# The skip term D x of a state-space layer: from products with diagonal matrices on TensorE to a copy on ScalarE and a product and a sum on GpSimd

## The chip, the cores and the metric

The kernel runs on one core of one Trainium2 chip. The metric is the device time of one execution in microseconds (us), the median of three runs. A profile of one further execution is at hand. Its engines are called PE (TensorE's matrix products; PEld is its loading of the stationary operand), DVE (VectorE), ACT (ScalarE), POOL (GpSimd) and SP (SyncE, which here only issues DMAs).

## What is computed

Two transformer-like layers over x of shape 4 x 512 x 512, all in float32. Each half layer is x = x + f(g), where g is a gate computed by scans over time (a bidirectional WKV recurrence) and f is in turn a state-space layer (Mamba2), a mixture of 8 experts, attention, and a feed-forward layer. The change lies in the state-space layer, whose core is this (b rows, l tokens, 16 heads of 64 channels, 1024 inner channels, 128 states):

```python
x = xBC[..., :D_INNER].reshape(b, l, NHEADS, HEADDIM)
xdt = xc * dtc[..., None]
Y_diag = jnp.einsum('bcgls,bgHcls,bcsgHp->bclgHp', CB, Lmat, xdt)
states = jnp.einsum('bcsgn,bgHcs,bcsgHp->bcgHpn', Bc, decay_states, xdt)
Y_off = jnp.einsum('bclgn,bcgHpn,bgHcl->bclgHp', Cc, prev, jnp.exp(dA_cs))
y = (Y_diag + Y_off).reshape(b, l, NHEADS, HEADDIM) + x * D_skip[None, None, :, None]
y = y.reshape(b, l, D_INNER)
y = y * jax.nn.silu(z)
```

and then a norm over the 1024 channels and a projection back to 512. The skip term is `x * D_skip`: each head's channels times one number of that head.

## The kernel before

**Stages.** The kernel first makes the gates of the first row. Then comes the state-space stage, which ends in the profile at about 720 us and overlaps the experts from about 660 us; then the experts, attention, and the feed-forward layer. During the state-space stage a generator (`make_gates`, stepped by `pump`) interleaves the gate work of seven further gates: scans on VectorE (L259, L265), products on VectorE (L254 to L331), exponentials and scalings on ScalarE. The gates are due one by one, where `have(...)` stands, the last two tiles before the end of the stage.

**Tiles, halves and groups.** The stage loops over 4 rows of the batch (`b`) and, in each, over 4 tiles of 128 tokens (`t`). Within a tile the 1024 channels are worked in two halves (`hh`) of 512, which are 8 heads. One tile's half is called a group here; there are 32. For each group the code calls

- `decays(u, hh)`: ScalarE makes the decay matrix `lm` of 8 heads (eight Relu at L1162, one Exp), VectorE multiplies it by `cb` (L1168), TensorE turns the convolved channels `xc`, which lie channel by token, into token by channel (`pxt`, four transposes, L1173), VectorE reads `pxt` twice for `xdt` and `xde` (L1177, L1181). Last, TensorE opens the sum `pyd` with four products of `xc` by `skip` (L1186); `skip` holds 8 diagonal 128 x 128 matrices with D on the diagonal, which GpSimd builds once at the start (L957).
- `outputs(u, hh)`: `pyo`, the product with the state (L1200), VectorE's scaling of it into `y` (L1201), eight products that end the sum `pyd` (L1203), VectorE's sum `y + pyd` (L1213), GpSimd's product by the gate `zs` (L1214). In a row's first tile there is no state, and one product on VectorE of `pyd` by `zs` (L1211) takes the place of these. Then the state is updated: `pst` (L1217), GpSimd's `st*ex` (L1222), VectorE's sum (L1223).
- `squares`, `norm`, `turn`, `project`, `scale`, `add_x`: the norm and the projection, one tile later, as `old`. `norm` is a chain of small GpSimd operations (L1232 to L1248) with one on VectorE (L1242).

**Order.** The code of one tile is written in the order `decays(u, 1)`, `outputs(u, 0)`, the norm of the tile before, `start_tile` and `start_scores` of the next, `decays(next, 0)`, `outputs(u, 1)`. The framework turns this text ahead of time into a fixed order for each engine, taking what stands earlier in the text first; `after(...)` holds some calls behind the last instruction of an engine. On the chip each engine then works through its own queue.

**Buffers.** Tiles with one tag share a ring of `bufs` buffers, and the next taker waits for the last reader of the oldest one. PSUM has three rings: `mm` (4 banks), `tp` (2 banks: transposes, `pxt` among them, and small products) and `acc` (2 banks: `pyd`, and the experts' `po`). In SBUF the rings of `xdt` and `xde` have 2 buffers, `y` has 3.

**Constants.** `cols` holds vectors as columns (one number per partition), `rows` holds vectors that are broadcast to all partitions; `heads(row, hh)` stretches 8 numbers, one per head, over 8 x 64 channels. Each of the two is loaded by one DMA on SP.

Of the kernel before, what the change touches and what calls it, by code (L numbers as in the profile page):

```python
# [10 lines left out]
F32 = mybir.dt.float32  # L11
# [3 lines left out]
ALU = mybir.AluOpType  # L15
# [3 lines left out]
P = 128  # L19
# [5 lines left out]
DI, DS, NH, HD, KC = 1024, 128, 16, 64, 4  # L25
CONV = DI + 2 * DS
NCV = CONV // P
NDI = DI // P
DPROJ = 2 * DI + 2 * DS + NH

E, I = 8, 512
# [27 lines left out]
    ("conv_w", NCV * KC),  # L59
    ("conv_b", NCV),  # L60
    ("norm_w", NDI),
    ("D_skip", NDI),
    ("gate_s", NFF),
    ("up_s", NFF),
    ("down_s", NC),
# [5 lines left out]
    _n += _w  # L71
NCOLS = _n

_ROWS = [("dt_bias", NH), ("A_log", NH), ("gate_b", E)]
_ROW = {}
_n = 0
for _name, _w in _ROWS:
# [6 lines left out]
def block_kernel(ctx: ExitStack, tc: tile.TileContext, a: dict, out: bass.AP):  # L84
    nc = tc.nc
# [51 lines left out]
    rt = ctx.enter_context(tc.tile_pool(name="moe_r", bufs=1))  # L137
# [11 lines left out]
    def ps_acc(name):  # L149
        return ps.tile([P, 512], F32, tag="acc", name=name, bufs=2)  # L150
# [7 lines left out]
    def col(name, i=0, n=1):  # L158
        lo = _COL[name][0] + i
        return cols[:, lo : lo + n]  # L160
# [5 lines left out]
    ident = const.tile([P, P], F32, name="ident")  # L166
# [307 lines left out]
    e_nq = count("e_nq", [[NQ, E]])  # L474
    v_id = count("v_id", [[1, 1]], 1)

    v_lo = rt.tile([P, 1], F32, name="v_lo")
    v_e = rt.tile([P, 1], F32, name="v_e")
    jk = rt.tile([P, E], F32, name="jk")
    nc.vector.tensor_tensor(jk, sel, e_nq, ALU.mult)  # L480
    nc.vector.tensor_reduce(v_e, jk, AX.X, ALU.add)
# [415 lines left out]
    with ExitStack() as ph:  # L897
# [3 lines left out]
        wz = ph.enter_context(tc.tile_pool(name="ssm_wz", bufs=1, reuse_waits="tile"))  # L901
        hp = ph.enter_context(tc.tile_pool(name="ssm_h", bufs=1, reuse_waits="tile"))
        sm = ph.enter_context(tc.tile_pool(name="ssm", bufs=1, reuse_waits="tile"))
# [48 lines left out]
        wzt = wz.tile([P, NC, DI], F32, name="wzt")  # L952
        wot = wz.tile([P, NDI, C], F32, name="wot")

        skip = wz.tile([P, NDI, P], F32, name="skip")
        for j in range(NDI):
            nc.gpsimd.tensor_scalar(skip[:, j, :], ident, col("D_skip", j), None, ALU.mult)  # L957
        for k in range(NC):
            nc.sync.dma_start(out=wxb[:, k, :], in_=a["in_projT"][k * P : (k + 1) * P, DI:])
        for k in range(NC):  # L960
# [170 lines left out]
        def start_scores(u):  # L1131
            w, t = u.w, u.t
            pp = ps_tp("pp")

            nc.tensor.matmul(pp[:, P : 2 * P], lhsT=w.Bc[:, u.tok], rhs=w.Cc[:, u.tok], start=True, stop=True)
            nc.tensor.transpose(pp[:, 2 * P : 3 * P], w.Bc[:, u.tok], ident)
            u.cb = sm.tile([P, P], F32, tag="cb", name="cb")
            nc.vector.tensor_tensor(u.cb, pp[:, P : 2 * P], tri_le, ALU.mult)
            u.bt = sm.tile([P, P], F32, tag="bt", name="bt", bufs=2)
            nc.scalar.copy(u.bt, pp[:, 2 * P : 3 * P])  # L1140
            u.ex, u.dte = w.ex[:, :, t, :], w.dte[:, t, :]
            u.ss = sm.tile([P, 2], F32, tag="ss", name="ss", bufs=2)
            u.xdt, u.xde, u.lm, u.pyd, u.y = [], [], [], [], []

        def load_sums(w, t, hh):

# [7 lines left out]
        def decays(u, hh):  # L1154

            w, t = u.w, u.t
            lm = w.lm.pop((t, hh))
            u.lm.append(lm)

            for i in range(8):  # L1160
                h = t * NH + hh * 8 + i
                nc.scalar.activation(  # L1162
                    lm[:, i, :], lm[:, i, :], AF.Relu, bias=w.cs[:, h : h + 1], scale=-1.0
                )
            lmf = lm.rearrange("p h l -> p (h l)")
            act(lmf, lmf, AF.Exp, scale=-1.0)
            for q in (slice(0, 4), slice(4, 8)):
                nc.vector.tensor_tensor(  # L1168
                    lm[:, q, :], lm[:, q, :], u.cb.unsqueeze(1).to_broadcast([P, 4, P]), ALU.mult
                )  # L1170
            pxt = ps_tp("pxt")
            for j in range(4):
                nc.tensor.transpose(  # L1173
                    pxt[:, j * P : (j + 1) * P], w.xc[hh * 4 + j][:, u.tok], ident
                )
            xdt = sm.tile([P, 512], F32, tag="xdt", name="xdt", bufs=2)
            nc.vector.tensor_tensor(split(xdt), split(pxt), heads(w.dt[:, t, :], hh), ALU.mult)  # L1177
            u.xdt.append(xdt)
            if not u.last:
                xde = sm.tile([P, 512], F32, tag="xde", name="xde", bufs=2)  # L1180
                nc.vector.tensor_tensor(split(xde), split(pxt), heads(u.dte, hh), ALU.mult)  # L1181
                u.xde.append(xde)

            pyd = ps_acc("pyd")
            for j in range(4):
                nc.tensor.matmul(  # L1186
                    pyd[:, j * P : (j + 1) * P], lhsT=w.xc[hh * 4 + j][:, u.tok],
                    rhs=skip[:, hh * 4 + j, :], start=(j == 0), stop=False,
                )
            u.pyd.append(pyd)  # L1190

        def outputs(u, hh):

            w, pyd = u.w, u.pyd[hh]
            ch = slice(hh * 512, (hh + 1) * 512)
            y = sm.tile([P, 512], F32, tag="y", name="y", bufs=3)
            u.y.append(y)
            if not u.first:
                pyo = ps_mm("pyo")
                nc.tensor.matmul(pyo, lhsT=w.Cc[:, u.tok], rhs=w.state[:, ch], start=True, stop=True)  # L1200
                nc.vector.tensor_tensor(split(y), split(pyo), heads(u.ex[:, 0, :], hh), ALU.mult)  # L1201
            for hd in range(8):
                nc.tensor.matmul(  # L1203
                    pyd[:, hd * HD : (hd + 1) * HD],
                    lhsT=u.lm[hh][:, hd, :],
                    rhs=u.xdt[hh][:, hd * HD : (hd + 1) * HD],
                    start=False,
                    stop=(hd == 7),
                )
            if u.first:  # L1210
                nc.vector.tensor_tensor(y, pyd, u.zs[hh], ALU.mult)  # L1211
            else:
                nc.vector.tensor_tensor(y, y, pyd, ALU.add)  # L1213
                nc.gpsimd.tensor_tensor(y, y, u.zs[hh], ALU.mult)  # L1214
            if not u.last:
                pst = ps_mm("pst")
                nc.tensor.matmul(pst, lhsT=u.bt, rhs=u.xde[hh], start=True, stop=True)  # L1217
                st = w.state[:, ch]
                if u.first:
                    nc.scalar.copy(st, pst)  # L1220
                else:
                    nc.gpsimd.tensor_tensor(split(st), split(st), heads(u.ex[:, 2, :], hh), ALU.mult)  # L1222
                    nc.vector.tensor_tensor(st, st, pst, ALU.add)  # L1223
# [75 lines left out]
        w = start_row(0)  # L1299
# [23 lines left out]
        u = start_tile(w, 0)  # L1323
# [6 lines left out]
        for b in range(B):  # L1330
# [6 lines left out]
            for t in range(NT):  # L1337
# [97 lines left out]
                old, u = u, nxt  # L1435
# [433 lines left out]
def _lay_out(n):  # L1869


    def chunks(v):

        return np.asarray(v).reshape(-1, P).T

    t = lambda v: np.ascontiguousarray(np.swapaxes(np.asarray(v), -1, -2))
    wkv = ("L0_cond", "L0_cond2", "L1_cond", "L1_cond2")
    w1, b1 = np.asarray(n["L0_ffn_w1"]), np.asarray(n["L0_ffn_b1"])
    cols = {
        "wkv_w": np.concatenate([chunks(n[f"{c}_w"]) for c in wkv], 1),  # L1880
        "wkv_u": np.concatenate([chunks(n[f"{c}_u"]) for c in wkv], 1),
        "condT": np.asarray(n["cond_512"]).T,
        "conv_w": np.asarray(n["L0_attn_conv_w"]).reshape(NCV, P, KC).transpose(1, 0, 2).reshape(P, -1),
        "conv_b": chunks(n["L0_attn_conv_b"]),
        "norm_w": chunks(n["L0_attn_norm_w"]),
        "D_skip": chunks(np.repeat(np.asarray(n["L0_attn_D_skip"]), HD)),
        "gate_s": chunks(n["L1_ffn_gate_s"]),
        "up_s": chunks(n["L1_ffn_up_s"]),
        "down_s": chunks(n["L1_ffn_down_s"]),
    }  # L1890
    rows = {
        "dt_bias": n["L0_attn_dt_bias"],
        "A_log": n["L0_attn_A_log"],
        "gate_b": n["L0_ffn_gate_b"],
    }
    by_part = lambda v: v.reshape(E, -1, P, v.shape[-1]).swapaxes(1, 2)
    w1x = np.stack([by_part(t(w1[:, i::2, :])) for i in range(2)], 2)
    got = {
        "cols": np.concatenate([cols[k] for k, _ in _COLS], 1),
        "rows": np.concatenate([np.asarray(rows[k]) for k, _ in _ROWS]),  # L1900
        "xT": np.asarray(n["x"]).transpose(2, 0, 1),
        "fT": np.asarray(n["fside_BxSxS_0"]).transpose(2, 0, 1),
        "in_projT": t(n["L0_attn_in_proj_w"]),
        "out_projT": t(n["L0_attn_out_proj_w"]),
        "gate_wT": t(n["L0_ffn_gate_w"]),
        "w1x": w1x.reshape(E, P, -1),
        "w2x": by_part(t(n["L0_ffn_w2"])).reshape(E, P, -1),
        "b1x": np.concatenate([b1[:, 0::2], b1[:, 1::2]], 1),
        "b2x": n["L0_ffn_b2"],
        "w_q": n["L1_attn_w_q"],  # L1910
        "w_kv": n["L1_attn_w_kv"],
        "w_dense": n["L1_attn_w_dense"],
        "gateT": t(n["L1_ffn_gate_w"]),
        "upT": t(n["L1_ffn_up_w"]),
        "downT": t(n["L1_ffn_down_w"]),
    }
    return {k: np.ascontiguousarray(v) for k, v in got.items()}
# [18 lines left out]
```

## Time and profile before

| | |
|---|---|
| median of three runs | 2333.18 us (2331.7 to 2336.78) |
| the profiled execution's own time | 2336.05 us |
| its span in the profile | 2334.3 us |
| granted TensorE clock, mean | 0.981 |
| the skip products at L1186 | from 101.4 to 652.9 us |

In the profile a float32 product of two 128 x 128 operands shows as two records, so the four skip products of a group are eight. The end of a TensorE record is modelled and lies after the start of the next; what a product costs TensorE is therefore read from start to start. Rows of busy time by stretch give: start and end, length, then for PE, PEld, DVE, ACT and POOL the busy us and the number of instructions, then the granted TensorE clock, the DMA engines' busy share and GB/s. Rows on waits give who waited, for whom, the total in us, how often, and the longest. Rows on one tile or line give the least, median and greatest duration in ns, and when the first and last one started.

### The profile page before, as it was taken

How to read it: one execution, taken by the hardware profiler on the slowest of the kernel's cores; microseconds unless marked ns; L12 is line 12 of the kernel's file. 1: busy time of each engine (PE TensorE's matmuls, PEld its weight loads, DVE VectorE, ACT ScalarE, POOL GpSimd, SP SyncE). 2: the span in 40 equal slices, each digit the busy share in tenths (PEclk: the TensorE clock that was granted, in tenths of full speed). 3: DMA queues.
4: the chain of work that ended last, by engine and by line, in shares of the span. 5: the costliest groups of instructions: out<-in, count | busy, mean ns of one | idle time of the engine just before them, and what ended most of it. 6: DMA issues, size and time to landing. Idle time of an engine off the chain costs nothing.

```text
span 2334.3 us, 24564 instructions
## 1 busy us (share of the span) xinstructions
PE 2201.7 (94%) x8148; PEld 1283.5 (55%) x8148; DVE 1463.2 (63%) x2846; ACT 1037.2 (44%) x2095; POOL 283.8 (12%) x306
## 2 busy tenths in 40 slices
PE   2879999999999899999899999999999999999999
PEld 1545565565655444444455555555555555558887
DVE  8698989999634566665466656555555544457332
ACT  4475675766712333242345544443444333343222
POOL 4023242332221111112100000000000000000000
PEclk9888999999999999999999999999999999999999
DMA  7442341622424368977622111011100000041100
GB/s 264 163 135 68 104 159 55 207 92 73 171 78 180 131 224 317 355 255 255 233 68 81 46 37 50 28 32 45 50 28 14 10 28 1 1 167 37 37 19 19
DMA packets 87653, 251.76 MB, mean 108 GB/s; under 512 B 9632, under 2 KB 18208, under 8 KB 78112
## 3 DMA queue, kind: packets, MB, share of 16 engines
q1 hardware_dynamic: 78656, 224.43, 28.2%
q0 software_dynamic: 6560, 21.50, 2.7%
q10 hardware_dynamic: 2304, 4.20, 0.5%
q8 instruction: 67, 1.10, 0.2%
q14 instruction: 66, 0.54, 0.1%
HBM read 285.09 MB, written 55.18 MB: 146 GB/s over the span
## 4 chain that ended last, share of the span: by engine, by line
PE 43%; DVE 4%; ACT 3%; issue 0%; DMA 0%; ACTq 0%
PE pd L1670 9%; PE pq L1606 7%; PE pctx L1655 6%; PE psc L1623 4%; PE pv L1592 2%; PE pk L1584 2%; PE ptp L1646 2%; PE pfo L1766 2%; PE pfo L1765 2%; PE pfg L1765 2%; PE pfg L1766 2%; PE pfu L1766 2%; PE pfu L1765 2%; DVE nmax L1628 1%; DVE num L259 1%; ACT pr L128 1%
## 5 line engine op out<-in xcount | busy, mean ns | idle before, releaser
L1606 PE MATMUL pq<-h,wq 128*128 128x512 f32 x512 | 245.5, 593 | 0.0
L1670 PE MATMUL pd<-cx,wd 128*128 128x512 f32 x512 | 223.0, 593 | 0.0
L1626 DVE TENSOR_TENSOR psc<-psc,mask 128x128 f32<-128x128 f32 x256 | 72.2, 287 | 191.7 <-PE psc L1623 191.3
L1048 PE MATMUL pc<-h,wxb 128*128 128x512 f32 x320 | 149.4, 623 | 43.6 <-DVE h L1307 38.7
L128 ACT ACTIVATE pr<-psc,nmax 128x128 f32<-128x128 f32 (+3 forms) x256 | 135.2, 529 | 104.0 <-DVE nmax L1628 103.0
L1678 DVE TENSOR_TENSOR xr<-xr,pd 128x512 f32<-128x512 f32 x64 | 44.0, 687 | 193.8 <-PE pd L1670 193.8
L1655 PE MATMUL pctx<-pT,v 128*128 128x512 f32 (+3 forms) x512 | 154.8, 446 | 8.4 <-ACT pT L1649 7.3
L1670 PEld LDWEIGHTS pd<-cx,wd 128*128 128x128 f32 x512 | 96.4, 191 | 115.1 <-issue 111.3
L1623 PE MATMUL psc<-kT,qT 128*128 128x128 f32 (+3 forms) x512 | 150.9, 435 | 3.2 <-ACT pr L128 2.4
L1655 PEld LDWEIGHTS pctx<-pT,v 128*128 128x128 f32 x512 | 94.4, 192 | 98.8 <-issue 38.4
L811 PE MATMUL pg<-w,hT 128*128 128x512 f32 x296 | 136.6, 603 | 6.8 <-ACT hT L784 6.8
L1614 ACT ACTIVATE qT<-pq 128x512 f32<-128x512 f32 x64 | 38.2, 598 | 233.6 <-PE pq L1606 233.6
L844 PE MATMUL po<-w,yT 128*128 128x512 f32 x296 | 135.8, 600 | 6.2 <-ACT yT L837 6.2
L822 PE MATMUL pn<-w,hT 128*128 128x512 f32 x296 | 133.4, 593 | 0.3 <-DMA w<-in_w1x 0.3
L1048 PEld LDWEIGHTS pc<-h,wxb 128*128 128x128 f32 x320 | 62.2, 199 | 116.2 <-issue 74.4
L1628 DVE TENSOR_REDUCE nmax<-psc 128x1 f32<-128x128 f32 (+3 forms) x256 | 123.4, 484 | 3.0
L1646 PEld LDWEIGHTS ptp<-ident,pr 128*128 128x128 f32 x640 | 77.7, 142 | 85.0 <-issue 41.6
L1606 PEld LDWEIGHTS pq<-h,wq 128*128 128x128 f32 x512 | 86.2, 191 | 53.6 <-issue 52.6
L1267 PE MATMUL po<-wot,yT 128*128 128x512 f32 x256 | 115.0, 603 | 0.0
L1119 PE MATMUL pz<-wzt,h 128*128 128x512 f32 x256 | 114.6, 596 | 0.3 <-ACT st L1220 0.3
L1623 PEld LDWEIGHTS psc<-kT,qT 128*128 128x128 f32 x512 | 86.2, 190 | 51.1 <-issue 25.8
L1646 PE MATMUL ptp<-ident,pr 128*128 128x128 f32 x640 | 96.1, 276 | 7.5 <-DVE pT L1649 4.0
(340 smaller groups left out, 4303.6 us busy)
## 6 DMA issues: line engine op xcount, KB each, us to landing
w<-in_w1x SPq DMA_DIRECT2D x76, 1024.0 KB
w<-in_w2x SPq DMA_DIRECT2D x38, 1024.0 KB
wb<-in_b1x SPq DMA_DIRECT2D x38, 512.0 KB
lm<-cs SPq DMA_DIRECT2D x32, 512.0 KB
kt<-in_fT SPq DMA_DIRECT2D x62, 256.0 KB
ek<-ek SPq DMA_DIRECT2D x62, 256.0 KB
ekv<-ekv SPq DMA_DIRECT2D x62, 256.0 KB
g<-num SPq DMA_DIRECT2D x30, 512.0 KB
```

Source lines behind the costliest of these rows:

```text
L128: nc.scalar.activation(*args, **kw)
L811: nc.tensor.matmul(pg, lhsT=hT[:, k, :], rhs=self.w1[s][0][:, k, :], start=(k == 0), stop=(k == NC - 1))
L844: nc.tensor.matmul(po, lhsT=yT[:, j, :], rhs=self.w2[s][:, j, :], start=(j == 0), stop=(j == NI - 1))
L1048: nc.tensor.matmul(pc, lhsT=wxb[:, k, m * P : (m + 1) * P], rhs=h[:, k, :], start=(k == 0), stop=(k == NC - 1),)
L1606: nc.tensor.matmul(pq, lhsT=u.wq[:, k, i * KVC : (i + 1) * KVC], rhs=u.h[:, k, :], start=(k == 0), stop=(k == NC - 1),)
L1623: nc.tensor.matmul(psc[:, :n], lhsT=qT[:, qi * P : n], rhs=u.kT[:, :n], start=True, stop=True)
L1628: nc.vector.tensor_reduce(nmax, psc[:, :n], AX.X, ALU.max, negate=True)
L1646: nc.tensor.transpose(ptp[:, kj * P : (kj + 1) * P], pr[:, kj * P : (kj + 1) * P], ident)
L1655: nc.tensor.matmul(pctx[:, kj * P :], lhsT=u.v[:, kj, :], rhs=pT[:, kj, kj * P :], start=(kj == 0), stop=(kj == NT - 1),)
L1670: nc.tensor.matmul(po, lhsT=u.wd[:, i, m * P : (m + 1) * P], rhs=u.ctxT[i], start=(i == 0), stop=(i == HPG - 1),)
L1765: nc.tensor.matmul(out_, lhsT=w, rhs=xs[0], start=first_, stop=False)
L1766: nc.tensor.matmul(out_, lhsT=w, rhs=xs[1], start=False, stop=last_)
```

## The change

The diagonal matrices go, and with them the four products of each group. Instead, in `decays`, ScalarE copies `pxt` from PSUM to a new SBUF tile `xs` (a ring of 2 buffers), and GpSimd multiplies it in place by D, broadcast over each head's channels. In `outputs`, GpSimd adds `xs` to `y` after VectorE's sum; in a row's first tile VectorE adds `xs` to `pyd`, where it multiplied `pyd` by `zs`. The product by `zs` is GpSimd's in every tile. `pyd` is taken from its ring in `outputs`, not in `decays`. D moves from `cols` (8 columns, repeated per channel) to `rows` (16 numbers, one per head). In SBUF, `skip` took 4 KB of a partition, and the two buffers of `xs` take 4 KB. `v_lo` and `v_e` of the routing become the two columns of one tile.

```diff
--- before.py
+++ after.py
@@ -59,7 +59,6 @@
     ("conv_w", NCV * KC),
     ("conv_b", NCV),
     ("norm_w", NDI),
-    ("D_skip", NDI),
     ("gate_s", NFF),
     ("up_s", NFF),
     ("down_s", NC),
@@ -71,7 +70,7 @@
     _n += _w
 NCOLS = _n
 
-_ROWS = [("dt_bias", NH), ("A_log", NH), ("gate_b", E)]
+_ROWS = [("dt_bias", NH), ("A_log", NH), ("D_skip", NH), ("gate_b", E)]
 _ROW = {}
 _n = 0
 for _name, _w in _ROWS:
@@ -474,8 +473,8 @@
     e_nq = count("e_nq", [[NQ, E]])
     v_id = count("v_id", [[1, 1]], 1)
 
-    v_lo = rt.tile([P, 1], F32, name="v_lo")
-    v_e = rt.tile([P, 1], F32, name="v_e")
+    v_both = rt.tile([P, 2], F32, name="v_both")
+    v_lo, v_e = v_both[:, 0:1], v_both[:, 1:2]
     jk = rt.tile([P, E], F32, name="jk")
     nc.vector.tensor_tensor(jk, sel, e_nq, ALU.mult)
     nc.vector.tensor_reduce(v_e, jk, AX.X, ALU.add)
@@ -952,9 +951,6 @@
         wzt = wz.tile([P, NC, DI], F32, name="wzt")
         wot = wz.tile([P, NDI, C], F32, name="wot")
 
-        skip = wz.tile([P, NDI, P], F32, name="skip")
-        for j in range(NDI):
-            nc.gpsimd.tensor_scalar(skip[:, j, :], ident, col("D_skip", j), None, ALU.mult)
         for k in range(NC):
             nc.sync.dma_start(out=wxb[:, k, :], in_=a["in_projT"][k * P : (k + 1) * P, DI:])
         for k in range(NC):
@@ -1140,7 +1136,7 @@
             nc.scalar.copy(u.bt, pp[:, 2 * P : 3 * P])
             u.ex, u.dte = w.ex[:, :, t, :], w.dte[:, t, :]
             u.ss = sm.tile([P, 2], F32, tag="ss", name="ss", bufs=2)
-            u.xdt, u.xde, u.lm, u.pyd, u.y = [], [], [], [], []
+            u.xdt, u.xde, u.lm, u.xs, u.y = [], [], [], [], []
 
         def load_sums(w, t, hh):
 
@@ -1180,18 +1176,14 @@
                 xde = sm.tile([P, 512], F32, tag="xde", name="xde", bufs=2)
                 nc.vector.tensor_tensor(split(xde), split(pxt), heads(u.dte, hh), ALU.mult)
                 u.xde.append(xde)
-
-            pyd = ps_acc("pyd")
-            for j in range(4):
-                nc.tensor.matmul(
-                    pyd[:, j * P : (j + 1) * P], lhsT=w.xc[hh * 4 + j][:, u.tok],
-                    rhs=skip[:, hh * 4 + j, :], start=(j == 0), stop=False,
-                )
-            u.pyd.append(pyd)
+            xs = sm.tile([P, 512], F32, tag="xs", name="xs", bufs=2)
+            nc.scalar.copy(xs, pxt)
+            nc.gpsimd.tensor_tensor(split(xs), split(xs), heads(row("D_skip"), hh), ALU.mult)
+            u.xs.append(xs)
 
         def outputs(u, hh):
 
-            w, pyd = u.w, u.pyd[hh]
+            w, pyd = u.w, ps_acc("pyd")
             ch = slice(hh * 512, (hh + 1) * 512)
             y = sm.tile([P, 512], F32, tag="y", name="y", bufs=3)
             u.y.append(y)
@@ -1204,14 +1196,15 @@
                     pyd[:, hd * HD : (hd + 1) * HD],
                     lhsT=u.lm[hh][:, hd, :],
                     rhs=u.xdt[hh][:, hd * HD : (hd + 1) * HD],
-                    start=False,
+                    start=(hd == 0),
                     stop=(hd == 7),
                 )
             if u.first:
-                nc.vector.tensor_tensor(y, pyd, u.zs[hh], ALU.mult)
+                nc.vector.tensor_tensor(y, u.xs[hh], pyd, ALU.add)
             else:
                 nc.vector.tensor_tensor(y, y, pyd, ALU.add)
-                nc.gpsimd.tensor_tensor(y, y, u.zs[hh], ALU.mult)
+                nc.gpsimd.tensor_tensor(y, y, u.xs[hh], ALU.add)
+            nc.gpsimd.tensor_tensor(y, y, u.zs[hh], ALU.mult)
             if not u.last:
                 pst = ps_mm("pst")
                 nc.tensor.matmul(pst, lhsT=u.bt, rhs=u.xde[hh], start=True, stop=True)
@@ -1883,7 +1876,6 @@
         "conv_w": np.asarray(n["L0_attn_conv_w"]).reshape(NCV, P, KC).transpose(1, 0, 2).reshape(P, -1),
         "conv_b": chunks(n["L0_attn_conv_b"]),
         "norm_w": chunks(n["L0_attn_norm_w"]),
-        "D_skip": chunks(np.repeat(np.asarray(n["L0_attn_D_skip"]), HD)),
         "gate_s": chunks(n["L1_ffn_gate_s"]),
         "up_s": chunks(n["L1_ffn_up_s"]),
         "down_s": chunks(n["L1_ffn_down_s"]),
@@ -1891,6 +1883,7 @@
     rows = {
         "dt_bias": n["L0_attn_dt_bias"],
         "A_log": n["L0_attn_A_log"],
+        "D_skip": n["L0_attn_D_skip"],
         "gate_b": n["L0_ffn_gate_b"],
     }
     by_part = lambda v: v.reshape(E, -1, P, v.shape[-1]).swapaxes(1, 2)
```

## The prediction

> **What bounds the kernel now.** I read the page's engine totals first, to see which engine fills the span; then busy time by stretch, because the change lives in one stage; then who waited for whom there; then single lines for the prices.
>
> ```profile
> PE 2201.7 (94%) x8148; PEld 1283.5 (55%) x8148; DVE 1463.2 (63%) x2846; ACT 1037.2 (44%) x2095; POOL 283.8 (12%) x306
> ```
>
> By this row TensorE is the bound and GpSimd nearly idle, which would make the change an easy gain. The row is an average, so the stretches come next (each engine's busy us; the skip products start at 101.4 and end at 653 us):
>
> ```profile
> 101.00:175.00 74.00, 58.85 (x227) 35.71 (x227) 61.05 (x76) 60.16 (x122) 13.28 (x13) 0.84 0.43 136
> 175.00:233.00 58.00, 56.24 (x212) 33.80 (x211) 47.85 (x81) 34.15 (x63) 18.61 (x14) 0.88 0.21 69
> 233.00:583.00 350.00, 336.62 (x1410) 200.42 (x1409) 326.61 (x539) 242.26 (x454) 109.72 (x107) 0.99 0.35 115
> 583.00:660.00 77.00, 75.84 (x394) 50.65 (x392) 48.77 (x120) 45.08 (x85) 19.30 (x31) 1.00 0.37 134
> ```
>
> In the 350 us stretch TensorE has 336.6 us of work and VectorE 326.6: two engines are full, not one. Only in the last stretch (48.8 of 77) does VectorE have room. Who waits for whom in the 350 us (VectorE's longest waits and its waits on TensorE, then TensorE's longest):
>
> ```profile
> DVE rs L1242 <- POOL rv L1236: 4.6, 5, 1.4
> DVE xc L1063 <- ACT xc L1059: 4.1, 3, 2.7
> ...
> DVE y L1211 <- PE pyd L1203: 1.5, 2, 1.0
> DVE cb L1138 <- PE pp L1136: 1.4, 1, 1.4
> DVE dtv L983 <- PE pdt L973: 1.3, 1, 1.3
> ...
> DVE cnt L557 <- PE pcnt L554: 0.7, 1, 0.7
> PE pot L1281 <- ACT o L1274: 4.4, 4, 1.7
> ```
>
> VectorE waited for TensorE for 1.5+1.4+1.3+0.7 = 4.9 us out of 350. Its remaining idle time is on ScalarE, GpSimd and DMA. A TensorE made faster can return to VectorE little more than those 4.9 us.
>
> **Removed.** There are 32 groups (16 tiles, two halves). One group on TensorE:
>
> ```profile
> 260.52 0.60 PE L1173 MATMUL pxt<-ident,xc 128*128 128x128 f32 x4
> 260.95 1.06 PE L1186 MATMUL pyd<-skip,xc 128*128 128x128 f32 x8
> 261.85 1.02 PE L1200 MATMUL pyo<-st,xc 128*128 128x512 f32 x2
> ```
>
> Start to next start, 261.85 - 260.95 = 0.90 us. 32 groups are 28.8 us (more at half clock: the group at 207 to 211 runs at 0.21 us a record). By the records' starts, 6 groups lie in 101-175, 2 in 175-233, 18 in 233-583, 6 in 583-660. The PSUM tile pyd is now taken when outputs begins, so two banks are held for a shorter time; TensorE waited 1.9 us on that ring once. Also gone: 8 GpSimd scalings at L957, 6.0 us, at 3 to 13.5 us, beside VectorE's first scans. I count them as 0, since nothing waits for GpSimd there. The two inputs change shape (cols 8 columns narrower, rows 16 wider) in the same two loads on SP; no DMA is added, removed or moved.
>
> **Added.** A copy on ScalarE, 32 times, nearest row the PSUM copy yT at L1259 (580 ns): 18.6 us on an engine busy 382 of 559 us. Three GpSimd operations replace one: the product by D (32; nearest form L1222, a product with a broadcast operand), the sum y+xs (24) and zs (8 more); nearest form L1214:
>
> ```profile
> L1214 POOL TENSOR_TENSOR y<-y,zs x24: 1262/1276/2191, 137.3 to 695.0; 128x512 f32<-128x512 f32 x24
> L1222 POOL TENSOR_TENSOR st<-st,ex x16: 1042/1046/1682, 122.8 to 648.0; 128x512 f32<-128x512 f32 x16
> ```
>
> At the medians: 32 x 1.046 + 32 x 1.276 = 74 us on GpSimd, busy 161 of 559. It fits; GpSimd does not become the bound. VectorE's own count stays: in the first tile of a row a product becomes a sum (L1211, 686 ns either way).
>
> **What it costs VectorE.** This is where the forecast is decided. The timeline:
>
> ```profile
> 321.21 0.68 DVE L1213 TENSOR_TENSOR y<-y,pyd 128x512 f32<-128x512 f32 x1
> 321.97 1.83 POOL L1214 TENSOR_TENSOR y<-y,zs 128x512 f32<-128x512 f32 x1 [5.12 <-DVE y L1213]
> 321.98 2.38 DVE L1168 TENSOR_TENSOR lm<-lm,cb 128x512 f32<-128x512 f32 x2
> ```
>
> Two lm products, 682 ns each at the median, took 2.38 us because a GpSimd product ran beside them; that product took 1.83 instead of 1.28. Each held the other up. Against their groups' quicker quarter, the VectorE instructions that met one of the 24 zs products were 10.7 us longer in all (0.45 us a product), those that met one of the 16 state products 2.7 us (0.17 us each). The two lengths differ because what follows is different: after L1213 VectorE often runs the state sum L1223, which reads PSUM and one SBUF operand, stays at 0.68 us and covers half of the product.
>
> The Trainium skill ("SBUF — State Buffer", section "Who interferes with whom") states the rule: VectorE's second SBUF read path is GpSimd's, an exclusive lock for a whole instruction; a VectorE instruction with two SBUF inputs and a GpSimd one that reads SBUF cannot overlap. It speaks against this change. Taken at its ceiling, every added operation stops VectorE for its length: 1.046 + 1.276 = 2.3 us a group, 42 us in the 350 us stretch. By the rows it is 0.17 + 0.45 = 0.62 us a group, 11 us. I take 0.9 us, nearer the rows: the sum y+xs uses up the cover of L1223, and zs, now 1.3 us later, meets whatever VectorE runs next. Of VectorE's time in this stretch 62% is in lines that read two SBUF operands (scans, gate products, lm).
>
> Other new waits. (1) The copy waits for a free xs buffer, that is, for the GpSimd sum two groups back; behind it on ScalarE are the next Relu and Silu, and it holds a transpose bank that L1258 and L1281 want. Today the transposes end less than 2 us after VectorE's y of two groups before in 5 groups of 30 (the second halves); there the copy is late by up to 2 us. (2) The product waits for the copy, and behind it in GpSimd's queue stand the norm's small steps, for which VectorE already waits 4.6 us (rs). (3) In a first tile VectorE's sum waits for the product, made half a tile earlier: 0. I put +2 us on all (0 to 10). The last groups' GpSimd work stands in the queue before the expert stage's gathers from 660 us: under 1 us.
>
> **The sum**, against the profiled execution (2336.05 us, span 2334.3), as a difference:
> - 101-233: 8 groups x 0.9 = +7. VectorE waited 11.8 us on TensorE here, at a throttled clock (0.84 to 0.88); half comes back, -6. Net +1.
> - 233-583: 18 x 0.9 = +16; relief 4.9 us of waits on TensorE and about 1 of the convolution's (part of the xc wait): -6. Net +10.
> - 583-660: TensorE full, VectorE at 63%. 6 x 0.9 = 5.4 us of TensorE come off in full: -5.4. The 5.4 us on VectorE lie in its 28 us of idle time; were that cover gone, they would cancel the gain.
> - after 660: the expert products share pyd's banks: -1. New waits: +2.
>
> Together +6.6. The profiled execution lies 2.9 us above the median of the runs (2333.18); I apply the difference to the median: 2339.8, so 2340.
>
> **The rivals.**
> A, faster: TensorE is the bound after all, as its 94% says. It decides if a group costs VectorE under about 0.5 us: then 18 groups cost 9 us, less than the 16.2 us that leave TensorE, and VectorE's 23 us of idle time must shrink to take the rest. For it: TensorE at 96% in that stretch, and 0.17 to 0.45 us an operation measured. Against it: 4.9 us of waits. With half of the 28.8 us kept: -12, so 2321; with nearly all, which would need VectorE's gate work to slip behind 583 us: -25, 2308.
> B, much slower: the lock at about 1.6 us a group (between 0.9 and the ceiling): 18 x 0.7 us more is +13, and GpSimd's queue delays the norm by some 5: 2358.
> C, no change that counts: TensorE's gain and VectorE's loss cancel, 2333. About 0.2% (4.7 us) is what a measurement of this kernel can tell from no change.
> That the products would stay under another name is excluded by the diff: no product with skip is left.
>
> **How the numbers follow.** My case (slower by 5 to 14 us, so 2338 to 2347) has 0.38, B 0.12, C 0.17, A 0.33, of which 0.08 for the near-full gain. Faster 0.33, same 0.17, slower 0.50. The range leaves out most of the near-full gain and the upper half of B: 2314 to 2358.
>
> **What would show it.** No L1186 products, TensorE's busy time 30 to 37 us lower, GpSimd's about 74 us higher plus what it waits for the lock. In the state-space stage VectorE's busy time must rise by 20 to 40 us at an unchanged count; lm, the scans and the den/num products carry it in their means, while the lines that read PSUM (L1177, L1201) keep 0.68 us. The stretch that was 233-583 should be longer, 583-660 shorter. I am wrong if VectorE's busy time rises by less than 15 us or its idle share falls far below 7% at a shorter stage (rival A), or if TensorE's new waits are on ScalarE's copy instead of VectorE.

## The result

The changed kernel takes 2368.82 us (median), against 2332.44 us for the kernel before on the same chip: ratio 1.0154, 95% interval 1.0137 to 1.0172, some 36 us slower. The forecast was 2340 (2314 to 2358): the direction held, but the time lies 11 us beyond the upper end of the range. The ratios are estimates over all runs and can differ a little from the quotient of two medians.

The page's totals after:

```profile
span 2367.3 us, 24158 instructions
PE 2208.9 (93%) x7892; PEld 1277.1 (54%) x7892; DVE 1492.8 (63%) x2846; ACT 1051.9 (44%) x2127; POOL 376.7 (16%) x362
```

VectorE (DVE) has the 2846 instructions that it had before, and is busy 29.6 us longer (1463.2 before). TensorE has 256 records fewer, and is not less busy but 7 us busier. Its granted clock shows in slices of 59 us (lowest line, in tenths of full speed):

```profile
PE   3869999899989999999989999999999999999999
PEclk9879979889899999999999999999999999999999
```

Within the state-space stage the clock falls again and again; the mean over the run is 0.963, before 0.981. Between 101 and 727 us it is 0.90 (0.96 before), and one product `po` of 128x512 lasts 633 ns at the mean (603 before): longer records make up for the missing ones. Busy time by stretch, the same stretches as before (PE, PEld, DVE, ACT, POOL, then the clock):

```profile
101.00:175.00 74.00, 51.31 (x182) 29.34 (x181) 65.57 (x75) 60.37 (x124) 32.51 (x23) 0.78 0.41 132
175.00:233.00 58.00, 57.60 (x195) 31.99 (x196) 50.98 (x83) 37.80 (x70) 27.42 (x19) 0.92 0.23 73
233.00:583.00 350.00, 324.59 (x1165) 186.19 (x1164) 314.95 (x495) 228.75 (x426) 145.07 (x133) 0.91 0.32 106
583.00:660.00 77.00, 71.33 (x304) 46.56 (x303) 57.78 (x86) 56.63 (x107) 36.48 (x34) 0.87 0.45 154
```

In the same 350 us VectorE now gets through 495 instructions, where it was 539, and TensorE 1165 records, where it was 1410 (144 of these were skip products). The stage falls behind: the last sum y + pyd starts at 694.2 us before and at 727.3 after, and from there to the end of the span both kernels need 1640 us. All of the loss lies in the stage. Between the first transposes pxt of successive rows, the first row takes 159.2 us before and 157.4 after; the second 147.6 and 161.6, the third 152.9 and 166.4. The fourth, to its last sum, takes 133.2 and 141.3.

A timeline of the changed kernel shows how GpSimd and VectorE meet:

```profile
596.17 1.72 POOL L1206 TENSOR_TENSOR y<-y,xs 128x512 f32<-128x512 f32 x1
...
596.68 1.76 DVE L1164 TENSOR_TENSOR lm<-lm,cb 128x512 f32<-128x512 f32 x1
...
597.96 1.61 POOL L1207 TENSOR_TENSOR y<-y,zs 128x512 f32<-128x512 f32 x1
```

The lm product (685 ns at the median) starts in the middle of the sum and takes 1.76 us: it ends 0.55 us after the sum, as if it had stood still until then. Then comes zs. The two lm lines, after and before (count, busy us, mean ns), show it in the mean:

```profile
L1164 DVE TENSOR_TENSOR lm<-lm,cb 128x512 f32<-128x512 f32 x64 | 46.6, 759 | 8.5 <-ACT lm L127 8.5
L1168 DVE TENSOR_TENSOR lm<-lm,cb 128x512 f32<-128x512 f32 x64 | 43.1, 706 | 6.4 <-ACT lm L128 6.3
```

The lines of y and xs (least, median, greatest ns):

```profile
L1207 POOL TENSOR_TENSOR y<-y,zs x32: 1261/1600/2861, 114.7 to 729.4; 128x512 f32<-128x512 f32 x32
L1206 POOL TENSOR_TENSOR y<-y,xs x24: 1258/1278/2189, 141.6 to 728.1; 128x512 f32<-128x512 f32 x24
L1180 ACT COPY xs<-pxt x32: 560/585/587, 108.6 to 690.0; 128x512 f32<-128x512 f32 x32
L1181 POOL TENSOR_TENSOR xs<-xs,rows x32: 1038/1043/2006, 109.3 to 690.6; 128x512 f32<-128x512 f32 x32
```

The median zs was 1276 ns before and is 1600 now: 20 of 32 took more than 1.4 us, where it was 5 of 24. In its new place behind the sum it meets VectorE's work more often. Counted as in the forecast (VectorE's instructions against their group's quicker quarter), those that met a zs product were about 19 us longer (11 before), those that met a sum about 10 us, those that met the product by D about 5 us. The shares are rough, because an instruction that met two operations is put down to one of them.

ScalarE shows a second thing. Its waits for pxt's other readers:

```profile
ACT xs L1180 <- DVE xde L1177: 14.2, 11, 2.7
...
ACT xs L1180 <- DVE xdt L1173: 9.7, 4, 3.7
```

All 32 copies start after VectorE's last read of the same PSUM tile, in the order in which the code names the readers. The timeline shows what that does in one place (the copy, then what stood behind it):

```profile
323.58 0.66 DVE L1173 TENSOR_TENSOR xdt<-pxt,dt 128x512 f32<-128x512 f32 x1
324.16 0.68 DVE L1177 TENSOR_TENSOR xde<-pxt,dte 128x512 f32<-128x512 f32 x1
...
324.93 0.58 ACT L1180 COPY xs<-pxt 128x512 f32<-128x512 f32 x1 [2.07 <-DVE xde L1177]
325.41 0.69 ACT L1267 ACTIVATE o<-po,rs 128x512 f32<-128x512 f32 x1
...
326.16 1.12 PE L1274 MATMUL pot<-ident,o 128*128 128x128 f32 x4 [4.05 <-ACT o L1267]
```

ScalarE idles 2.07 us at the copy, the scaling o behind it is late, and TensorE stands still for 4.05 us. TensorE's longest waits in the stage are on ScalarE (yT, o and bt) or on VectorE. Whether a copy stood ahead of ScalarE's work in each of them is not shown. After:

```profile
PE pp L1131 <- ACT yT L1252: 13.4, 4, 4.5
PE pyd L1195 <- DVE xdt L1173: 11.3, 6, 3.9
PE pdt L969 <- DVE h L403: 7.0, 1, 7.0
PE pot L1274 <- ACT o L1267: 6.4, 3, 4.0
PE pxt L1169 <- ACT bt L1136: 4.8, 2, 4.1
```

The longest before:

```profile
PE pc L1048 <- DVE h L404: 4.9, 1, 4.9
PE pp L1135 <- ACT yT L1259: 4.4, 3, 2.6
PE pot L1281 <- ACT o L1274: 4.4, 4, 1.7
```

### The profile page after: what moved, and what is told of

Same layout as the page of the kernel before. It is cut to its first block, busy times and chain, and to the rows that moved or that the text cites. A ratio compares the mean times of both kernels' runs of the same rounds, so it can differ in the third digit from the quotient of the medians.

```text
span 2367.3 us, 24158 instructions
## 1 busy us (share of the span) xinstructions
PE 2208.9 (93%) x7892; PEld 1277.1 (54%) x7892; DVE 1492.8 (63%) x2846; ACT 1051.9 (44%) x2127; POOL 376.7 (16%) x362
## 4 chain that ended last, share of the span: by engine, by line
PE 43%; DVE 4%; ACT 3%; issue 0%; DMA 0%; ACTq 0%
PE pd L1663 9%; PE pq L1599 7%; PE pctx L1648 6%; PE psc L1616 4%; PE pv L1585 2%; PE pk L1577 2%; PE ptp L1639 2%; PE pfo L1759 2%; PE pfo L1758 2%; PE pfg L1758 2%; PE pfg L1759 2%; PE pfu L1759 2%; PE pfu L1758 2%; DVE nmax L1621 1%; DVE num L258 1%; ACT pr L127 1%
## 5 line engine op out<-in xcount | busy, mean ns | idle before, releaser
L1260 PE MATMUL po<-wot,yT 128*128 128x512 f32 x256 | 121.5, 631 | 0.0
L1115 PE MATMUL pz<-wzt,h 128*128 128x512 f32 x256 | 121.1, 612 | 0.0
```

## The experiments

Four theories were put up. L: GpSimd's operations hold up VectorE on the shared way to SBUF. W: ScalarE's copy waits behind VectorE, and the queue behind it starves TensorE. Q: GpSimd's queue is longer, so zs and the norm come late. K: TensorE's pauses lower its clock, and that is part of the loss. Edits are against the changed kernel unless said otherwise; lines left out are marked by three dots. A microsecond figure beside a ratio is (ratio - 1) x 2332.

| run | ratio to before | 95% interval | us |
|---|---|---|---|
| the change | 1.0154 | 1.0137 to 1.0172 | +36 |
| e1 nothing in place of the skip products | 0.9982 | 0.9971 to 0.9993 | -4 |
| e2 copy only | 1.0030 | 1.0016 to 1.0043 | +7 |
| e3 GpSimd only | 1.0104 | 1.0062 to 1.0146 | +24 |
| e4 copy from a bank of its own | 1.0165 | 1.0132 to 1.0199 | +38 |
| e5 memsets, free to move | 0.9985 | 0.9965 to 1.0005 | -3 |
| e6 GpSimd's product only | 0.9996 | 0.9978 to 1.0013 | -1 |
| e7 copy from SBUF, free to move | 0.9988 | 0.9973 to 1.0004 | -3 |
| e8 before, less VectorE's xde | 1.0026 | 1.0008 to 1.0045 | +6 |
| e9 e1 and e8 together | 0.9940 | 0.9919 to 0.9961 | -14 |
| e10 before, with e3's GpSimd work | 1.0120 | 1.0071 to 1.0168 | +28 |
| e11 the sum on VectorE | 1.0136 | 1.0102 to 1.0170 | +32 |
| e12 TensorE kept busy | 1.0242 | 1.0213 to 1.0272 | +56 |
| e13 e2 from a bank of its own | 1.0026 | 1.0008 to 1.0043 | +6 |
| e14 the change, copy from SBUF | 1.0170 | 1.0134 to 1.0205 | +40 |
| e15 copy written first | 1.0200 | 1.0164 to 1.0236 | +47 |
| e16 memsets in place | 0.9990 | 0.9970 to 1.0010 | -2 |
| e17 copy from SBUF, in place | 1.0014 | 1.0000 to 1.0027 | +3 |

**What each comparison holds.** The framework can order the queues anew when the text changes, and the traces show where it did. There are three groups within which VectorE, ScalarE and TensorE run the same sequence, but for the instructions that the edit adds, removes or alters: e1, e3, e6 and e16 (two or three VectorE instructions have changed places in e3 and e16); e2 and the change; the kernel before and e10. In the other comparisons the order differs too: between before and e1 452 of VectorE's 2846 places hold another instruction, from 176 us on, between e1 and e2 430, from 107 us on. These differences contain the new order, and no run takes it apart.

**The change in its parts: e1, e2, e3.** Both added parts are taken out (e1), then each is put back alone.

```diff
-            xs = sm.tile([P, 512], F32, tag="xs", name="xs", bufs=2)
-            nc.scalar.copy(xs, pxt)
-            nc.gpsimd.tensor_tensor(split(xs), split(xs), heads(row("D_skip"), hh), ALU.mult)
...
             if u.first:
-                nc.vector.tensor_tensor(y, u.xs[hh], pyd, ALU.add)
+                nc.vector.tensor_tensor(y, pyd, u.zs[hh], ALU.mult)
             else:
                 nc.vector.tensor_tensor(y, y, pyd, ALU.add)
-                nc.gpsimd.tensor_tensor(y, y, u.xs[hh], ALU.add)
-            nc.gpsimd.tensor_tensor(y, y, u.zs[hh], ALU.mult)
+                nc.gpsimd.tensor_tensor(y, y, u.zs[hh], ALU.mult)
```

> The changed kernel with nothing put in place of the skip products: the skip term is left out of the computation, TensorE's 28.8 us are gone, ScalarE and GpSimd do what they did before. Theory W (the copy waits on ScalarE behind VectorE's two reads of pxt, what stands behind it is late, TensorE pauses and its clock falls) and theory L (GpSimd's added operations hold up VectorE): both expect a gain here, 2310 to 2328 us. Theory R (TensorE's relief is worth nothing, since VectorE bounds the stage and another order of the instructions costs the time): 2333 or more, and if the order is the cause, up to 2369.

> As the first run, and in addition ScalarE's copy of pxt to xs, which nothing reads; GpSimd's product and sum are left out, so the skip term is missing. Theory W: most of the loss is here, 20 to 35 us above the first run, with a granted clock in the state-space stage near the changed kernel's 0.91. Theory L: within 6 us of the first run.

> The changed kernel without ScalarE's copy: GpSimd's product reads xdt from SBUF instead, so that the skip term is D x dt and not D x; GpSimd's and VectorE's work are as in the changed kernel. Theory L: the loss stays, 2360 to 2370 us. Theory W: most of it goes, 2330 to 2345 us, and VectorE's busy time stays as high as in the changed kernel (1493 us).

The page's engine rows of e1 and of e3:

```profile
PE 2183.9 (94%) x7892; PEld 1258.0 (54%) x7892; DVE 1463.2 (63%) x2846; ACT 1036.8 (45%) x2095; POOL 285.5 (12%) x298
```

```profile
PE 2200.1 (93%) x7892; PEld 1266.9 (54%) x7892; DVE 1487.0 (63%) x2846; ACT 1037.7 (44%) x2095; POOL 375.6 (16%) x362
```

The removal of 28.8 us from TensorE gave 4 us, new order included; e1 also keeps the change's small edits (pyd taken later, D in `rows`). The copy costs 1.0030 - 0.9982, 11 us, again with a new order. GpSimd's work costs 1.0104 - 0.9982, 28 us, at the same order, and VectorE is 23.8 us busier with the same instructions. In e3 the product reads xdt, so it starts earlier than in the change. With the product in its real place, the change against e2, GpSimd's work costs 1.0154 - 1.0030, 29 us, and VectorE is 30.0 us busier (1462.8 us in e2). The parts add up: -4 + 11 + 28 = 35, measured 36. Theory L has the largest part; W expected e3 at 2345 at most, and it is 2356.

The equal order of e2 and the change allows a closer look. The same VectorE instruction starts later in the change by 9.4 us at 233 us, by 20.9 at 583 and by 28.0 at 660; VectorE's extra busy time up to it is 8.1, 23.5 and 27.7 us. So the delay grows with VectorE's longer instructions through the whole stage, and there is little left in this pair for another cause.

**Is it the reads, or the queue? e5, e16.** In e1's kernel GpSimd gets memsets, which read nothing. In e5 the framework moved them all ahead of 89 us, so it shows nothing on the stage. In e16 they are held in place: two where the product stood (not shown), two behind y's sum and ahead of zs:

```diff
...
+            nc.gpsimd.memset(y[:, 0:1], 0.0)
+            for _ in range(2):
+                with after(nc.gpsimd):
+                    nc.gpsimd.memset(u.xs[hh], 1.0)
...
```

> The first run's kernel (no skip term, no copy) with GpSimd filled as in the changed kernel, but by instructions that read nothing from SBUF: two memsets of 128x512 in place of the product and two in place of the sum, in the same places of the text. Theory L in its narrow form (what costs is GpSimd's and VectorE's shared way to SBUF reads): within 6 us of the first run's 2328, VectorE busy 1463 to 1467 us. Theory Q (it is GpSimd's longer queue, in which zs and the norm's steps come late): 2340 to 2357 us with VectorE's busy time unchanged.

> The fifth run again, with GpSimd's memsets held in their places, since there they ran before 89 us, ahead of the stage: two of 128x512 (about 1.04 us) behind the GpSimd instruction before the product's place, and in the sum's place one of a single column of y, which waits for VectorE's y, then two of 128x512, then zs. They read nothing from SBUF; the skip term is missing and one channel of y in each half is zeroed. Theory L in its narrow form: VectorE busy 1460 to 1468 us, 2325 to 2334 us. Theory Q (zs and the norm come late): 2340 to 2357 us at that busy time.

Two groups of GpSimd and the engine row, e16:

```profile
L1210 POOL MEMSET xs<- 128x512 f32 x64 | 34.1, 533 | 1.8
L1182 POOL MEMSET xs<- 128x512 f32 x64 | 33.5, 525 | 2.0
```

```profile
PE 2189.4 (94%) x7892; PEld 1263.9 (54%) x7892; DVE 1465.8 (63%) x2846; ACT 1037.5 (45%) x2095; POOL 346.4 (15%) x458
```

67.6 us of memsets, in these places, leave VectorE at 1465.8 us (1463.2 in e1) and the time at e1's within the intervals. Theory Q falls: zs comes late here too, and it costs nothing. What is left is the reads. The Trainium skill ("SBUF — State Buffer", section "Who interferes with whom") says so too: a GpSimd instruction that only writes does not stop a VectorE one with two SBUF inputs. The runs agree.

**Which of GpSimd's operations? e6, e11, e10.** e6 has the product alone. e11 gives the sum to VectorE:

```diff
-                nc.gpsimd.tensor_tensor(y, y, u.xs[hh], ALU.add)
+                nc.vector.tensor_tensor(y, y, u.xs[hh], ALU.add)
```

> GpSimd's product by D alone (it reads xdt; its result is read by nothing; the sum and the first tile's zs stay out, so the skip term is missing). The 28 us of the third run over the first are shared among 32 products, 24 sums and 8 first-tile zs. Theory L by the number of operations: 32 of 64, 14 us, so 2342. Theory L by what runs beside them (the product falls beside VectorE's reads of pxt, the sum and zs do not): 4 to 8 us, 2332 to 2336, with VectorE 4 to 8 us busier than in the first run. Theory Q: about 2328, since no product stands in y's chain.

> The changed kernel with the sum y+xs of the later tiles on VectorE (24 instructions of two SBUF inputs, about 0.68 us, 16 us of VectorE) and not on GpSimd. Theory L: GpSimd's sum and the zs that it pushes later cost VectorE some 21 us by the traces, so that VectorE's busy time is the same or lower, and the time 2358 to 2369 us: VectorE could as well have done it itself. If GpSimd's sum were nearly free: 2375 to 2386 us.

The product alone costs 0.0014, 3 us, and the intervals overlap: half of GpSimd's added instructions, a ninth of their cost at most by these medians. VectorE is busy 1466.9 us, 3.7 more than in e1. In e6 the product starts when VectorE has made xdt and goes on to read pxt for xde: 22 of the 24 xde ran beside a product, and they took 666 to 685 ns, no longer than elsewhere. In the change the product comes later, behind the copy, and costs VectorE about 5 us. In e11, on VectorE, the sums are 24 more instructions of 684 ns at the median, and the result is not told apart from the change (1.0136 and 1.0154). VectorE is busy 1495.5 us with the sums and 1492.8 us without them: GpSimd's sum costs VectorE about what it costs when VectorE does it.

> The kernel before with its skip products kept on TensorE (by the identity, so D is 1) and GpSimd's product, sum and first-tile zs of the third run on top (the product reads xdt and takes another row of 16 numbers). If the parts add up: 28 us above before, 2360. If the lock hits only a stage whose bound is VectorE, and TensorE's work in place covers part of it: 15 to 22 us, 2349 to 2356. Dearer than 28 us if TensorE and VectorE now fill each other's gaps.

In e10 the skip products stay (rhs=ident in place of skip) with e3's GpSimd work on top: +28 us, what e3 costs above e1, though the interval is wide (17 to 39 us). VectorE's busy time, 1492.7 us, is 29.5 above before's, at the same order. So the lock costs this much with TensorE's relief and without it, as far as the intervals tell.

**Why was TensorE's relief worth so little? e8, e9, e12.** In e8 and e9 xde is not formed, and u.xde.append(xdt) takes its place.

> The kernel before with its skip products on TensorE, less VectorE's 24 products xde (the state is formed from xdt, a different sum): 16.3 us off VectorE, nothing off TensorE. If VectorE's time is the stage's time (the reading under which 28.8 us off TensorE were worth 4): 2316 to 2323 us. If both engines are full and each needs the other's relief: 2327 to 2333 us.

> The first run's kernel (no skip term at all) less VectorE's 24 products xde as in the eighth run (the state is formed from xdt): 28.8 us off TensorE and 16.3 us off VectorE. Theory B (both engines were full, each alone gives nothing): 2308 to 2318 us, 10 us or more below the first run's ratio of 0.998. Theory K (TensorE's own pauses and the clock that falls after them eat the relief): about the first run's time, 2323 to 2332, with a granted clock at or below 0.975. If the sum of the two single results holds: +1, so 2335.

Relief of VectorE alone gave nothing by the end of the run: the kernel was 6 us slower (VectorE's busy time fell by 12 us, not 16; why the time rose is not settled). Both together gave 14 us. That fits two full engines, each of which returns time only when the other is relieved too. It is not shown, because in all three kernels the order of the queues differs from before's. e9 leaves out work that must be done, so it is no version to use.

The traces, each of one execution, say where relief was lost. (e1's ended 10.4 us ahead of before's, where the medians differ by 4.) By the sum y + pyd at 298 us, e1 was 8.8 us ahead of before; by the one at 368 us it was 0.7 behind. e16, at e1's order, shows a like loss (6.3 ahead, 3.4 behind). After 583 us e1 gained again. e8 too was ahead at first, by 10.1 us at 221 us. In e1 three things come together there. TensorE, now ahead, waits once 3.9 us for VectorE's gate product h. Its granted clock is 0.93 from 298 to 321 us and 0.83 from there to 341, where it was 1.00 before. And between 322 and 367 us VectorE's order differs almost throughout. Over the stage, e1's waits for h (before: 4.9, 1, 4.9):

```profile
PE pc L1044 <- DVE h L403: 14.4, 3, 8.0
```

Which of the three took the time is open.

e12 fills TensorE's pauses in the changed kernel:

```diff
+            fill = ps_acc("fill")
+            for m in range(NC):
+                nc.tensor.matmul(fill, lhsT=ident, rhs=wot[:, m, :], start=True, stop=True)
             pot = ps_tp("pot")
```

> The changed kernel with four more products of 128x512 on TensorE per tile, of constants, read by nothing, just ahead of the transposes pot, where TensorE waits for ScalarE: 16 x 1.7 = 27 us more work. Theory K (pauses halve the clock, and that is part of the loss): the granted clock rises from 0.963 to 0.970 or more and the time stays within 8 us of the changed kernel, or falls below it. Without that effect: 2380 to 2396 us.

The clock rose from 0.963 to 0.973 as theory K wanted, and the time rose by 20 us for 27 us of work (an estimate, 16 tiles at 1.7 us). Making the clock higher in this way did not pay. Theory K is neither shown nor excluded by it, since the added work costs time of its own and the order changed. For the lock theory K is not needed, as the pair e2 and change shows; for the rest it stays open.

**Why does the copy cost 11 us? e4, e13, e7, e17, e14, e15.** e4 (the full change) and e13 (e2) feed the copy from four more transposes into a tile of the acc ring:

```diff
-            nc.scalar.copy(xs, pxt)
+            pxs = ps_acc("pxs")
+            for j in range(4):
+                nc.tensor.transpose(
+                    pxs[:, j * P : (j + 1) * P], w.xc[hh * 4 + j][:, u.tok], ident
+                )
+            nc.scalar.copy(xs, pxs)
```

> The changed kernel, but the copy has a PSUM tile of its own (four more transposes a group into the acc ring, about 0.44 us a group on TensorE, 14 us in all), so that it need not wait for VectorE's reads of pxt. Theory W: 15 to 25 us below the changed kernel in spite of 14 us more on TensorE, 2343 to 2354 us. Theory L: at or above the changed kernel, 2366 to 2380 us.

> The second run's kernel (copy alone, no GpSimd additions, no skip term), with the copy fed by a PSUM tile of its own as in the fourth run (14 us of transposes more on TensorE). If the wait for VectorE's reads of pxt is what the copy costs: 2326 to 2334 us, below the second run's 2339.6 in spite of TensorE. If any copy out of PSUM here makes ScalarE wait (then for TensorE): 2338 to 2350.

Neither was faster than its counterpart, but each also carries an estimated 14 us more of TensorE work. ScalarE then waited elsewhere (waits of e13):

```profile
ACT xs L1185 <- PE pxs L1182: 21.1, 10, 4.9
```

A copy from SBUF waits for no engine in these traces. In e7 the framework gathered most of these copies at the changes of rows; in e17 each is held behind its group's Exp:

```diff
-            nc.scalar.copy(xs, pxt)
+            with after(nc.scalar):
+                nc.scalar.copy(xs, w.xc[hh * 4])
```

> The second run's kernel, but ScalarE copies 128x512 of the convolved channels, long there in SBUF, not pxt: the same time on ScalarE and no wait for VectorE (the skip term is missing). Theory W: the 11.5 us of the copy go, 2326 to 2331 us. Theory S (ScalarE's own time costs, 18.6 us in the queue ahead of what others wait for): 2336 to 2342 us.

> The seventh run again, with ScalarE's copy of 128x512 from the convolved channels in SBUF held right behind the Exp of its group, since there the copies ran in bunches at the change of rows. No wait for VectorE or TensorE; the skip term is missing. Theory W (the wait at the head of ScalarE's queue is the cost): 2326 to 2333 us. Theory S (0.58 us of ScalarE in that place, 32 times, is the cost, wait or not): 2336 to 2342 us, like the copy from PSUM.

e7: 1 us above e1. e17: 7 us above e1, 4 us below the copy from PSUM, and the intervals of e17 and e2 overlap. So ScalarE's own 0.6 us in a busy place may be more of the copy's cost than its wait, but the two are not told apart, and the order differs in each of these runs. The loss is not even either: e2 is level with e1 until 448 us (+0.5 us) and 9.9 us behind at 511. There TensorE waits once 3.8 us for ScalarE's o, and its granted clock is 0.76 between 480 and 500 us (0.91 in e1). Gathered at the changes of rows (e7), the same copies cost next to nothing.

> The changed kernel complete on GpSimd and VectorE, but ScalarE copies 128x512 of the convolved channels from SBUF (the wrong layout, so the skip term is wrong), with nothing to wait for. If the copy's wait adds to the lock: 2355 to 2361 us, about the third run's. If the two overlap, and the lock alone sets the time: 2364 to 2370.

> The changed kernel with ScalarE's copy written ahead of VectorE's two reads of pxt, nothing left out. If the order of the three readers of one PSUM bank is kept as written, VectorE now waits for ScalarE: ScalarE's wait for VectorE goes to nearly 0, VectorE waits up to 0.58 us a group, 18 us. As VectorE is the fuller engine: 2368 to 2385 us. If ScalarE's wait was the dearer one: 2355 to 2366.

e14 was no better than the change. Another wait came in: the copy, early now, waited for a free xs buffer, that is for GpSimd's sum (waits of e14):

```profile
ACT xs L1180 <- POOL y L1206: 26.7, 7, 6.3
```

and the product, no longer tied to pxt, made VectorE's instructions about 16 us longer, where it was about 5. In e15 the copy stands ahead of VectorE's reads, and VectorE, the fuller engine, waits:

```profile
DVE xdt L1175 <- ACT xs L1173: 13.0, 5, 8.2
```

The median is 11 us above the change; the two intervals just overlap.

## Why the prediction was right or wrong

- **What TensorE's relief returns: 6 + 6 + 5.4 us, and 1 for the banks.** This is the step that failed most: 18 forecast, 4 measured (e1). I read VectorE's waits on TensorE and returned half or all of them, as if each queue kept its order and a wait that ends were not replaced by another. At first the time did come back (8.8 us by 298 us); then it was lost again, where TensorE waited for VectorE, its clock was lower and VectorE's order was another. Which of these did it stays open.
- **The new waits, +2 us.** This step failed too: the copy costs 11 (e2 against e1). I named the ring of xs and the banks, and missed that the copy comes behind VectorE's two reads of the same PSUM tile, and that 0.58 us of ScalarE, 68% busy, may not be free in that place. How the 11 us divide between wait, copy and new order is open. The ring wait that I named did appear, in e14.
- **What of the lock's price reaches the time.** The forecast let 5.4 us of it vanish in VectorE's idle time after 583 us and charged 23. Measured 28 (e3 against e1, e10 against before) and 29 (the change against e2). The idle time hid nothing: from 583 to 660 us the change fell 7.1 us further behind e2.
- **The price of the lock on VectorE, 0.9 us a group, 28.8 us in all.** Right: VectorE's busy time rose by 29.6 us at an unchanged count. So was the place: lm's mean rose from 706 to 759 ns, xdt and y<-pyo,ex kept 0.68 us. That the two totals agree to a microsecond is luck, since 0.9 was picked between 0.62 by the rows and the ceiling of 2.3, without a sum over the three operations. The product is nearly free alone; the sum and the zs behind it are dear. The direction of the forecast rests on this step, and e3, e10 and e16 show it.
- The differences are 14 us for the relief, 9 for the copy and 5 for the lock: 28 of the 29 us between 2340 and 2369.
- **The bound, two engines full.** VectorE was no free engine: the lock's 28 us show that. That the stage has two bounds fits e1, e8 and e9, but the new orders leave it unproven.
- **TensorE's busy time 30 to 37 us lower.** Wrong. It rose by 7 us, at a lower clock and with longer records. In e1, without the new waits, it fell by 17.8 us.
- **The stretch after 583 us shorter.** Wrong: the fourth row, which holds it, took 8.1 us more. The sign that I had given for being wrong, TensorE's new waits on ScalarE, came in part: its wait for yT rose from 4.4 to 13.4 us.
- **Rivals.** A (TensorE is the bound) and C (no change) are refuted by the result, and e1 does not bear A out: with no work put in its place, the gain is 4 us. B, at 2358, came nearer than my case, but put all of its excess on the lock and on GpSimd's queue; the lock cost 28 us, and e16 shows no cost of the queue.

## What to carry to other kernels

When two engines are each above 90% busy in a stage, don't count on getting back the time taken off one of them: here it was 4 of 28.8 us, while work that blocked the other was paid in full. Before moving work, leave it out in a trial, and see what its absence is worth. In such trials compare the order of the queues in the traces: where it is the same, a difference belongs to the edit; where the framework chose another, it holds that too. Work moved to an idle GpSimd was not free when it read SBUF beside a full VectorE; beside VectorE's reads out of PSUM it nearly was. A copy of 0.6 us, 32 times, cost between 1 and 11 us with its place and source (e7, e17, e2), so the place wants as much thought as the length.

## What the runs showed that I had not expected

67.6 us of memsets on GpSimd can cost nothing (e16), and 90 us of reading operations 28 us (e3). Filling TensorE's pauses raised its clock by a hundredth and lost 20 us (e12). And 16 us of products off VectorE, alone, made the kernel no faster (e8).
